# When keys are asked for, and how far behind its transfer a reciprocal stands: an attention and feed-forward kernel on Trainium2

## The chip, the cores and the metric

The kernel runs on one core of a Trainium2 chip. The metric is device time in microseconds (us), the median of some runs; one further execution is profiled. TensorE (PE in the profile) multiplies matrices, VectorE (DVE) reduces and does elementwise work, ScalarE (ACT) evaluates functions, GpSimd (POOL) does elementwise work too, and SyncE (SP) issues nearly all DMAs. Each engine works through its own list of instructions in order, and waits for the others through semaphores.

## The reference

4096 rows of width 256 go through two sandwich layers, in 32-bit floats:

```python
x = x + layernorm(attention(layernorm(x)))      # 16 heads of 16, causal softmax, projection
x = x + layernorm(ffn(layernorm(x)))
# ffn(h): silu(h @ w1.T * s1) * (h @ w2.T * s2)   256 -> 1024
#         gelu(. @ h1.T * sh1), gelu(. @ h2.T * sh2)   1024 -> 1024 twice
#         . @ w3.T * s3                                1024 -> 256
```

Attention is over all 4096 rows, each row with those up to itself. The feed-forward weights are -1, 0 or 1, with a scale for each output.

## The kernel before

**Attention in items.** The rows are cut into 8 blocks of 512 (QB), the heads into 4 groups of 4 (G). An item (j, g) is one query block with one group of heads; there are 32, in the order (0,0), (0,1) and so on. Item (j, g) has 4(j+1) steps, one for each 128 keys (`kt`), so 576 steps in all; a normal one takes about 2.7 us. A step asks for keys (`ask`), takes a pair of units of the row maxima (products `pm` L508 on TensorE, maxima L521 and L525 on DVE), two score units (products `s` L591, exponential L606 on ACT, the causal mask L611 on POOL on the diagonal), the product with the values of an earlier step (`av` L641), and then some pieces of background work. The maxima of an item are found up to two items ahead of its scores, so the `pm` products need its keys that early. The `pm` products write banks that come free only when DVE has reduced them.

**The order of the work** is written out by hand: inside a `manual_schedule`, each engine's instructions stand in the order in which the code issues them, and an engine that waits holds up all that comes behind it. The same goes for SP and its DMAs.

**Keys.** Keys and queries of a block are computed by `prep`, split into a high and a low half, and written to memory (L389, 256 KB each, from SP; the destination's outermost dimension has 8 rows of heads). For each item they are loaded again in the form that the products want. `chunks` lists all pairs (item, key block) in order; `keys` loads the next one of the list (two DMAs of 256 KB, L396) into a ring of 16 slots, each of two tiles. Chunk c of item (j, g) holds the 512 keys of block c for group g. Queries are loaded at an item's start, two items ahead.

**Background.** `prep(j + 2)` is added at step 2 of item (j, 0), `project(j)` when the last group of block j has been weighed; both are generators, and each `yield` ends a piece. `bg.pace` shares the pieces that are left out over the steps that are left; PREP, PROJECT and NORM are the numbers of pieces it counts with. A `yield Background.BESIDE` lets a further unit of maxima stand beside a background matmul. 88 pieces of weight rounding (`halve_weights`, L677 to L696) go in between.

**project(j)** (from L185) loads the block's x, and the softmax sums from the stored weighed values (L191, as soon as the last group's store, L652, has landed). Some pieces later DVE takes their reciprocal (L194), in the next piece it is stored (L196) and loaded again broadcast over the rows of a head (L200 to L204, beside the weighed values `oT`); some pieces later POOL multiplies (L208), one product in a piece; two pieces on the projection's matmuls `py` (L218), the bias on DVE (L226) and the statistics follow, then the normalisation on POOL and the store of x1 (L240).

**Feed-forward.** `feed_forward` (from L848) goes over the 8 blocks: 8 output chunks of w1 and w2 (`za`, `zb`, L940, L959, L961), then 8 chunks of h1 and 8 of h2 (`z`, L940, L974), each followed on DVE by a split into high and low halves (L910, L911), and at last w3 (`pyf`, L987). `project(7)` and after it `norm_block(1)` are background of block 0: one piece after each w1/w2 chunk, two after each h1/h2 chunk:

```python
                        bg.step()
                        if j == 0:
                            bg.step()
```

`norm_block` takes statistics (L142), adds epsilon (`ve`, L143), raises to the power -0.5 on POOL (`rstd`, L145), normalises on DVE (`yn`, L149), and in the next piece transposes on TensorE (`ptf`, L260).

Of the kernel before, what the change touches and what calls it, by code (L numbers as in the profile page):

```python
# [19 lines left out]
NT = QB // P  # L20
# [47 lines left out]
def sandwich_kernel(  # L68
# [39 lines left out]
    def rows(src, j):  # L108
        return src[j * QB : (j + 1) * QB, :].rearrange("(t p) d -> p t d", p=P)

    def load_block(j, src=x):
        t = xpool.tile([P, NT, D], F32, tag="x", name=f"x{j}")
        nc.sync.dma_start(out=t, in_=rows(src, j))
        return t
# [21 lines left out]
    def layernorm_stats(src, mv, t):  # L136
        st = stat.tile([P, nc.vector.BN_STATS_DIM], F32, tag="bn", name="bn")
        nc.vector.bn_stats(st, src)
        nc.vector.bn_aggr(mv[:, t, :], st)

    def layernorm_rstd(mv):
        ve = stat.tile([P, NT], F32, tag="ve", name="ve")  # L142
        nc.vector.tensor_scalar_add(ve, mv[:, :, 1], EPS)  # L143
        rstd = stat.tile([P, NT], F32, tag="rstd", name="rstd")
        nc.gpsimd.tensor_tensor(rstd, ve, neghalf, ALU.pow)  # L145
        return rstd

    def normalize(dst, src, mv, rstd, t, engine=nc.vector):
        engine.tensor_scalar(  # L149
            dst, src, mv[:, t, 0:1], rstd[:, t : t + 1], ALU.subtract, ALU.mult  # L150
        )
# [28 lines left out]

    weighed = [scratch.tile([G, P, QB], F32, tag=f"av_{j}", name=f"avd_{j}") for j in range(NB)]
    inverse = [scratch.tile([H, QB], F32, tag=f"inv_{j}", name=f"invd_{j}") for j in range(NB)]
    PREP, PROJECT, NORM = 22, 20, 12

    def project(j, room):  # L185

        xj = load_block(j)

        sums = stat.tile([P, H * QB // P], F32, tag="sums", name=f"sums_{j}")
        heads = weighed[j].rearrange("g (h e) n -> (g h) e n", e=HW)  # L190
        nc.sync.dma_start(out=sums, in_=heads[:, HD, :].rearrange("h (a n) -> h a n", a=8))  # L191
        for _ in range(3):
            yield True
        nc.vector.reciprocal(sums, sums)  # L194
        yield True
        nc.sync.dma_start(out=inverse[j].rearrange("h (a n) -> (h a) n", a=8), in_=sums)  # L196
        oT, inv = room.features(j)
        for c in range(DC):
            mine = slice(8 * c, 8 * (c + 1))
            nc.sync.dma_start(out=oT[:, c, :], in_=heads[mine, 0:HD, :])  # L200
            nc.sync.dma_start(
                out=inv[:, c, :],
                in_=inverse[j][mine, None, :].to_broadcast([8, HD, QB]),
            )  # L204
        for _ in range(4):
            yield True
        for c in range(DC):
            nc.gpsimd.tensor_tensor(oT[:, c, :], oT[:, c, :], inv[:, c, :], ALU.mult)  # L208
            yield True
        for _ in range(2):  # L210
            yield True
        y = room.tokens(j)
        mv = stat.tile([P, NT, 2], F32, tag="mv", name=f"mvy_{j}")
        for half in range(0, NT, 2):
            ps = room.bank(f"py_{j}_{half}").rearrange("p (t f) -> p t f", t=2)
            for t in range(2):
                for c in range(DC):
                    nc.tensor.matmul(  # L218
                        ps[:, t, :],
                        lhsT=oT[:, c, (half + t) * P : (half + t + 1) * P],  # L220
                        rhs=wp[:, c, :],
                        start=(c == 0),
                        stop=(c == DC - 1),
                    )
                yield Background.BESIDE
            nc.vector.tensor_tensor(  # L226
                y[:, half : half + 2, :],
                ps,
                bp[:, None, :].to_broadcast([P, 2, D]),
                ALU.add,  # L230
            )
            for t in range(2):
                layernorm_stats(y[:, half + t, :], mv, half + t)
            yield True
        rstd = layernorm_rstd(mv)
        for t in range(NT):
            normalize(y[:, t, :], y[:, t, :], mv, rstd, t, nc.gpsimd)
            nc.gpsimd.tensor_tensor(y[:, t, :], y[:, t, :], xj[:, t, :], ALU.add)
            yield True
        nc.sync.dma_start(out=rows(x1[j], 0), in_=y)  # L240
        yield True
# [36 lines left out]
    with ExitStack() as actx:  # L278
# [114 lines left out]
        def load_rows(tag, name, key, j, h):  # L393

            t = (piece if key == "k" else query)(tag, name, F32R)
            nc.sync.dma_start(  # L396
                out=t.bitcast(F32),
                in_=halves_of[key, j][h : h + 2].rearrange("h a b d n -> (h a b d) n"),
            )
            return t  # L400
# [11 lines left out]
        chunks = [(n, c) for n in range(G * NB) for c in range(n // G + 1)]  # L412
        RING = 2 * NB
        kT, asked = {}, [0]

        def keys(n, c):

            for pr in range(2):
                kT[n, c, pr] = load_rows(
                    f"k{asked[0] % RING}_{pr}", f"k{n}_{c}_{pr}", "k", c, 4 * (n % G) + 2 * pr  # L420
                )
            asked[0] += 1

        def ask(n, kt):

            while asked[0] < len(chunks) and chunks[asked[0]][0] <= n + 2:
                if asked[0] >= RING and chunks[asked[0] - RING] >= (n, (kt - 1) // NT):
                    return
                keys(*chunks[asked[0]])

        xTs = {}

# [189 lines left out]
        class Values:  # L622
# [9 lines left out]
            def step(self, now):  # L632
                if not self.queue or self.queue[0][0] > now:
                    return
                _, j, g, kt, q0, es = self.queue.popleft()
                last = NT * (j + 1) - 1
                if self.av is None:
                    self.av = ps_av.tile([P, QB], F32, tag="av", name=f"av_{j}_{g}")
                for h in range(4):
                    o = (4 * g + h) * VW  # L640
                    nc.tensor.matmul(  # L641
                        self.av[h * HW : (h + 1) * HW, q0:],
                        lhsT=vb[kt // NT][:, kt % NT, o : o + HW],
                        rhs=es[h // 2][:, h % 2, q0:],
                        start=(kt == 0),
                        stop=(kt == last),
                    )
                if kt == last:
                    av_sb = wk1.tile([P, QB], F32, tag="av_sb", name=f"av_sb_{j}_{g}")
                    nc.scalar.copy(av_sb, self.av)  # L650
                    self.av = None
                    nc.sync.dma_start(out=weighed[j][g], in_=av_sb)  # L652
                    if g == G - 1 and j < NB - 1:
                        bg.add(("project", j), project(j, room), PROJECT)
# [122 lines left out]
        for n, (j, g) in enumerate(items):  # L777
# [22 lines left out]
            for kt in range(count[n]):  # L800
                ask(n, kt)
                if (g, kt) == (0, 2) and j + 2 < NB:
                    bg.add(("prep", j + 2), prep(j + 2), PREP)
                due = begun + (goal - begun) * (kt + 1) // count[n] - issued
                pairs = [next(stream) for _ in range(due)]
                issued += due
                es = []
                if pairs:
                    issue(MaxUnit(*pairs[0][0]))
                es = [  # L810
                    issue(ScoreUnit(j, g, kt, pr, not pairs and next(alone)))
                    for pr in range(2)
                ]
                if pairs:
                    issue(MaxUnit(*pairs[0][1]))
                values.step(now + 1)
                for pair in pairs[1:]:
                    for args in pair:
                        issue(MaxUnit(*args))
                now += 2  # L820
                values.add(j, g, kt, max(kt - NT * j, 0) * P, es, now - 1)
                rows_of(now)
                bg.pace(count[n] - kt + count[n] * max(G - 2 - g, 0))
                if j > 0 and kt % 4 == 2 and kt < NT * j:
                    next(halving, None)
# [22 lines left out]
    def feed_forward(halves):  # L848
# [6 lines left out]
        with ExitStack() as fctx:  # L855
# [93 lines left out]
            room, bg = Room(), Background()  # L949
            keep_features(0)([xT0[:, c, :] for c in range(DC)])  # L950
            bg.add("project", project(NB - 1, room), PROJECT)
            for j in range(NB):
                xT = xTs[j]
# [91 lines left out]
```

## Time and profile before

| what | value |
|---|---|
| time, three runs | 2571.3, 2574.32, 2575.26 us; median 2574.32 |
| the profiled execution's own time | 2574.63 us |
| its span in the profile | 2572.9 us |
| PE busy | 95% |
| DVE, ACT, POOL busy | 71%, 49%, 22% |
| mean granted clock of TensorE | 0.966 |
| loads of keys, L396 | 288 of 256 KB |

The span runs from the first to the last instruction; the execution's time is 1.7 us more. Lines named L... are those of the kernel before; from L426 on the changed kernel's are two higher. In a line of the timeline stand the start and the length in us, the engine (PEld is a weight load, SPq a DMA's issue on SP), the line, the operation, output and input by name, the shapes and the number of instructions; in square brackets how long the engine had been idle before and what released it. The granted clock is the share of TensorE's full speed that its throttle gave.

### The profile page before, as it was taken

The numbers are of one execution on the slowest core, as the hardware profiler recorded it, in microseconds if no ns is written. First come the engines' busy times: TensorE is split into PE (matmuls) and PEld (weight loads), VectorE is DVE, ScalarE is ACT, GpSimd is POOL, SyncE is SP. The second block draws the span as 40 slices with busy tenths as digits, with TensorE's granted clock in tenths as the row PEclk, the third lists the DMA queues.
The fourth block names the chain that finished last, engine by engine and source line by source line (L and its number), as shares of the span: only waits on it lengthen the run. The fifth ranks groups of instructions, "written<-read, shape, count | busy, mean of one in ns | idle before, by whom it ended". The sixth has DMA issues, their size and how long they took to land. (4 is left out here: it accounts for less than half of the span.)

```text
span 2572.9 us, 40118 instructions
## 1 busy us (share of the span) xinstructions
PE 2439.2 (95%) x15237; PEld 1444.8 (56%) x15237; DVE 1824.1 (71%) x3965; ACT 1257.2 (49%) x1490; POOL 575.2 (22%) x869
## 2 busy tenths in 40 slices
PE   5899999999999999999999999999989999999998
PEld 2454445445445544554455554544468877887786
DVE  2687788879788987898899898986055445544553
ACT  1335466556566655666577666766712222222221
POOL 2325333332242234322322222000120000000000
PEclk8779899899999999999999999999999999999999
DMA  4444244232233323324212232111120000000000
GB/s 156 144 152 154 88 135 153 99 129 74 91 108 123 120 83 130 109 79 141 66 62 95 83 96 72 57 45 55 42 90 17 17 1 17 17 17 1 17 9 10
DMA packets 134777, 202.73 MB, mean 79 GB/s; under 512 B 14864, under 2 KB 59536, under 8 KB 134576
## 3 DMA queue, kind: packets, MB, share of 16 engines
q1 hardware_dynamic: 132624, 198.75, 23.3%
q8 instruction: 122, 2.00, 0.3%
q10 hardware_dynamic: 1776, 1.18, 0.2%
q0 software_dynamic: 176, 0.15, 0.1%
q14 instruction: 79, 0.65, 0.1%
HBM read 137.91 MB, written 62.13 MB: 78 GB/s over the span
## 5 line engine op out<-in xcount | busy, mean ns | idle before, releaser
L606 ACT ACTIVATE e<-s 128x1024 f32<-128x1024 f32 (+3 forms) x1175 | 1040.6, 936 | 618.5 <-PE s L591 611.5
L521 DVE TENSOR_REDUCE mx<-pm 128x1 f32<-128x512 f32 x1792 | 1112.4, 682 | 160.4 <-PE pm L508 145.8
L508 PE MATMUL pm<-k,q 64*128 64x512 f32 (+3 forms) x2304 | 636.8, 460 | 56.8 <-DVE mx L521 40.7
L508 PEld LDWEIGHTS pm<-k,q 64*128 64x128 f32 x2304 | 326.5, 190 | 567.3 <-DVE mx L521 394.7
L641 PE MATMUL av<-e,v 128*32 128x512 f32 (+3 forms) x4608 | 591.1, 584 | 2.9 <-POOL e L611 2.9
L591 PE MATMUL s<-q,k 64*128 64x512 f32 (+3 forms) x2304 | 476.3, 395 | 7.6 <-DVE y L226 3.1
L591 PE MATMUL s<-mrow,ones 64*128 64x512 f32 (+3 forms) x2304 | 461.6, 384 | 0.0
L525 DVE CUSTOM_DVE_ANT_0 pm<-pm,mask 128x384 f32<-128x384 f32 (+3 forms) x512 | 239.8, 517 | 75.3 <-PE pm L508 71.4
L974 ACT ACTIVATE fb<-z,sh 128x512 f32<-128x512 f32 x128 | 88.1, 688 | 396.6 <-PE z L940 377.8
L591 PEld LDWEIGHTS s<-q,k 64*128 64x128 f32 x2304 | 237.0, 191 | 79.0 <-issue 19.3
L591 PEld LDWEIGHTS s<-mrow,ones 64*128 64x128 f32 x2304 | 241.8, 191 | 38.6 <-DVE mrow L565 0.7
L611 POOL TENSOR_SCALAR_AFFINE_SELECT e<-e 128x256 f32<-128x256 f32 x256 | 102.2, 407 | 647.6 <-ACT e L606 645.9
L145 POOL TENSOR_TENSOR rstd<-ve,neghalf 128x4 f32<-128x4 f32 x32 | 32.9, 1027 | 847.7 <-DVE ve L143 822.1
L940 PE MATMUL z<-hb_0h,h 128*128 128x512 f32 x512 | 203.7, 398 | 0.0
L940 PE MATMUL z<-hb_0l,h 128*128 128x512 f32 x512 | 202.2, 395 | 0.0
L641 PEld LDWEIGHTS av<-e,v 128*32 128x32 f32 x4608 | 92.6, 109 | 148.8 <-issue 130.0
L910 DVE CAST hb_1h<-fb 128x512 fp32r<-128x512 f32 x64 | 27.4, 428 | 149.9 <-ACT fb L974 149.9
L910 DVE CAST hb_0h<-fb 128x512 fp32r<-128x512 f32 x64 | 27.5, 430 | 139.4 <-ACT fb L974 139.4
L940 PEld LDWEIGHTS z<-hb_0h,h 128*128 128x128 f32 x512 | 96.8, 189 | 22.9
L940 PEld LDWEIGHTS z<-hb_0l,h 128*128 128x128 f32 x512 | 96.8, 189 | 22.1
L959 ACT ACTIVATE sl<-za,s 128x512 f32<-128x512 f32 x64 | 44.1, 689 | 131.4 <-DVE fa L961 66.4
L693 POOL CAST wh<-wc 128x256 fp32r<-128x256 f32 x88 | 34.9, 397 | 261.8 <-DMA wc<-in_h_t_dram 197.1
(235 smaller groups left out, 2430.9 us busy)
## 6 DMA issues: line engine op xcount, KB each, us to landing
k<-k SPq DMA_DIRECT2D x288, 256.0 KB
q<-q SPq DMA_DIRECT2D x64, 256.0 KB
x<-in_x_dram SPq DMA_DIRECT2D x16, 512.0 KB
k<-hik SPq DMA_DIRECT2D x32, 256.0 KB
k<-lok SPq DMA_DIRECT2D x32, 256.0 KB
q<-hiq SPq DMA_DIRECT2D x32, 256.0 KB
q<-loq SPq DMA_DIRECT2D x32, 256.0 KB
avd<-av_sb SPq DMA_DIRECT2D x32, 256.0 KB
```

Source lines behind the costliest of these rows:

```text
L508: nc.tensor.matmul(ps[:, 0:n], lhsT=qT[j, g][pr][r, t * P : (t + 1) * P], rhs=kT[G * j + g, c, pr][r, 0:n], start=True, stop=True,)
L521: nc.vector.tensor_reduce(self.mx[:, h, c : c + 1], ps[:, 0:n], AX.X, ALU.max)
L525: nc.vector.tensor_tensor_reduce(out=ps[:, 0:n], in0=ps[:, 0:n], in1=mask[:, QB - n : QB], scale=1.0, scalar=-3.0e38, op0=ALU.add, op1=ALU ...
L591: nc.tensor.matmul(self.ps[i][:, self.q0 :], lhsT=(self.k, ones[pr])[m][r, :], rhs=(qT[j, g][pr], mT[j, g])[m][r, self.q0 :], start=(m == ...
L606: nc.scalar.activation(e[:, at : at + n, q0:], ps[:, :, q0:], AF.Exp)
L611: nc.gpsimd.affine_select(out=at, in_=at, compare_op=ALU.is_ge, fill=0.0, base=0, pattern=[[0, 2], [1, P]], channel_multiplier=-1,)
L641: nc.tensor.matmul(self.av[h * HW : (h + 1) * HW, q0:], lhsT=vb[kt // NT][:, kt % NT, o : o + HW], rhs=es[h // 2][:, h % 2, q0:], start=(k ...
L693: nc.gpsimd.tensor_copy(hi, w)
L910: nc.vector.tensor_copy(hi, full)
L940: nc.tensor.matmul(ps, lhsT=w[c], rhs=single(part[:, c, :]), start=(c == 0 and i == 0), stop=(c == kc - 1 and i == parts - 1),)
L959: nc.scalar.activation(sl, za, AF.Silu, scale=s1[:, oc : oc + 1])
L974: nc.scalar.activation(h, z, AF.Gelu, scale=sc[:, oc : oc + 1])
```

## The change

`ask` no longer asks at each step for all chunks that the ring and the limit of two items ahead allow; it asks at even steps alone, and for one chunk. In `project`, two more pieces stand between the load of the sums and the reciprocal, and one more between the loads of the weighed values and the product; PROJECT counts the three.

```diff
-    PREP, PROJECT, NORM = 22, 20, 12
+    PREP, PROJECT, NORM = 22, 23, 12
...
         nc.sync.dma_start(out=sums, in_=heads[:, HD, :].rearrange("h (a n) -> h a n", a=8))
-        for _ in range(3):
+        for _ in range(5):
             yield True
         nc.vector.reciprocal(sums, sums)
         yield True
...
-        for _ in range(4):
+        for _ in range(5):
             yield True
         for c in range(DC):
             nc.gpsimd.tensor_tensor(oT[:, c, :], oT[:, c, :], inv[:, c, :], ALU.mult)
             yield True
...
         def ask(n, kt):
 
-            while asked[0] < len(chunks) and chunks[asked[0]][0] <= n + 2:
-                if asked[0] >= RING and chunks[asked[0] - RING] >= (n, (kt - 1) // NT):
-                    return
-                keys(*chunks[asked[0]])
+            at = asked[0]
+            if kt % 2 or at == len(chunks) or chunks[at][0] > n + 2:
+                return
+
+            if at < RING or chunks[at - RING] < (n, (kt - 1) // NT):
+                keys(*chunks[at])
```

## The prediction

> **What bounds it now.** First the page's busy row, then the list of waits, then the timeline around those waits.
>
> ```profile
> PE 2439.2 (95%) x15237; PEld 1444.8 (56%) x15237; DVE 1824.1 (71%) x3965; ACT 1257.2 (49%) x1490; POOL 575.2 (22%) x869
> ```
>
> TensorE works 95% of the span, so only what shortens or makes a TensorE gap, or slows its clock, moves the end. The waits that touch the edit:
>
> ```profile
> DVE sums L194 <- DMA sums<-avd: 21.0, 7, 7.6
> PE pm L508 <- DVE mx L521: 40.7, 62, 3.9
> ```
>
> (Columns: total us, count, longest.) The reciprocal waits 21.0 us for its transfer, and TensorE waits for DVE's maxima. Block 6 shows that they are one thing:
>
> ```profile
> 1189.52 0.32 SPq L652 DMA_DIRECT2D avd<-av_sb  x1
> ...
> 1194.17 0.39 PE L508 MATMUL pm<-k,q 64*128 64x512 f32 x1
> ...
> 1194.71 0.58 SPq L191 DMA_DIRECT2D sums<-avd  x1
> ...
> 1197.29 0.55 DVE L194 RECIPROCAL sums<-sums 128x64 f32<-128x64 f32 x1 [4.46 <-DMA sums<-avd]
> ...
> 1198.44 0.79 PE L508 MATMUL pm<-k,q 64*128 64x512 f32 x1 [3.88 <-DVE mx L521]
> ```
>
> The sums are read only once the last group's store has landed; DVE stands 4.46 us at the reciprocal, the pm banks behind it stay full, and TensorE stands 3.88. The like stands at 280.6, 447.5, 654.5 and 904.5 us: 3.36+1.09+2.45+0.86+3.88 = 11.6 us. The clock drops afterwards:
>
> ```profile
> 653.00:667.00 14.00, 11.55 (x66) 5.07 (x68) 7.62 (x20) 5.98 (x7) 4.86 (x6) 0.76 0.52 169
> 1192.00:1206.00 14.00, 10.12 (x60) 4.70 (x60) 7.19 (x16) 5.77 (x7) 3.99 (x5) 0.76 0.66 197
> ```
>
> (Window, us, busy PE, PEld, DVE, ACT, POOL, then granted clock, DMA share, GB/s.) A clock of 0.76 over 14 us is 3.4 us lost in each; 280 to 292 has 0.86, 1.7 us. Part lies in the gaps themselves: against 2.7 us of a normal step, the steps at these places are 19.5 us too long together, 7 to 8 beyond the gaps. I take 7.0, a choice between 4 and 8.5.
>
> [...] 0.50 in the slices after 1194, while the 0.86 us gap costs no clock. [...]
>
> **The change, part by part.** All engines keep their program order, so the built order tells where things land.
>
> *Reciprocal two pieces later, in attention.* It moves 8 to 9 DVE instructions down for five of the seven projections, 13 and 6 for two, and 4 for the first: about two steps, 5.4 us. The longest wait is 4.46, so all vanish: +11.6 us, and the clock +7.0. The second (447) could keep up to 1 us. Cover is the maxima and stats between; without it the 4.46 stays. The product, one piece later again, waits on POOL (22% busy) for its transfer; the y matmuls come three pieces later and x1 is needed much later: nothing.
>
> *The same in the last projection, in the feed-forward.*
>
> ```profile
> 1874.30 0.40 PE L940 MATMUL zb<-xTf_0l,w 128*128 128x512 f32 x1
> ...
> 1876.94 0.55 DVE L194 RECIPROCAL sums<-sums 128x64 f32<-128x64 f32 x1 [7.63 <-DMA sums<-avd]
> ...
> 1878.12 0.51 PE L940 MATMUL z<-ha_0h,h 128*128 128x512 f32 x1 [3.42 <-DVE fa L961]
> ```
>
> The sums land at about 1876.9 behind weights whatever DVE does. Two more w1/w2 chunks (DVE .75+.43+.69 = 1.87 us each) go first: the wait is 7.63-3.74 = 3.9, and TensorE's 3.42 gap, with its clock loss, goes: +3.7. Further on:
>
> ```profile
> 1924.38 1.03 POOL L145 TENSOR_TENSOR rstd<-ve,neghalf 128x4 f32<-128x4 f32 x1 [12.27 <-DVE ve L143]
> ...
> 1926.01 2.21 PE L260 MATMUL ptf<-ident,yn 128*128 128x128 f32 x8 [3.75 <-DVE yn L149]
> ```
>
> In block 0 two pieces run after each h1/h2 chunk. Normalising is piece 27 and the transposes 28, in one pair, so nothing covers rstd 1.03 plus four yn of .35. Three pieces later they are 30 and 31, in different pairs: a chunk of 3.7 us (16 matmuls of .23) comes between, against a chain of 4.4 (activation .69, casts .43+.69, ve .16, rstd 1.03, yn 1.4) to 5.0 with stats of .6 ahead of it: 0.7 to 1.3 stay, I take 1.1. Lost before: 3.75, about 1.2 of the slow 2.21 [...], and 1 of clock after it = 5.9. +4.8. If both pieces fell in one pair again, nothing would be gained here.
>
> *Keys asked for by one chunk in every second step.* Before, an item's first step asks for all that the ring allows up to two items ahead. Comparing each load's place in SP's order with its first use, all later chunks keep 10 us or more of lead, save these.
>
> Place A, item (0,2). The second chunk of (1,0) is asked for at step 0 before (106 us, ahead of prep(2)'s writes); after, at step 2, behind 12 of them. In TensorE's order its first product comes right after pq.
>
> ```profile
> 120.55 1.88 PE L366 MATMUL pq<-xT,wqk 128*128 128x512 f32 x4
> ...
> 122.36 0.33 PE L508 MATMUL pm<-k,q 64*128 64x128 f32 x2
> ...
> 125.90 2.98 SPq L389 DMA_DIRECT2D q<-hiq  x2
> ...
> 128.97 2.50 SPq L389 DMA_DIRECT2D q<-loq  x2
> ```
> ```profile
> 120.00:138.00 18.00, 17.06 (x101) 9.51 (x99) 8.67 (x29) 7.66 (x13) 7.85 (x12) 1.00 0.52 194
> 138.00:158.00 20.00, 18.80 (x79) 9.30 (x77) 15.14 (x46) 4.08 (x7) 2.44 (x6) 0.50 0.57 199
> ```
>
> TensorE is there at 122.4. SP gets to the keys at 131.5. The 12 writes are 3.15 MB; at 194 to 200 GB/s, begun at 117 and slow at first, they are through at 135.5; [...] Lower bound: landing 2 us after issue, 133.5, 11.1. Clock after it: an estimate of 3 (0 to 6), from the 3.4 lost after 3.88. A smaller one: (1,1)'s second chunk behind the store of 140.88, 1 us (0 to 2).
>
> Place B, item (1,2). The third chunk of (2,0) comes behind four writes of prep(3), its product directly after one that TensorE has before:
>
> ```profile
> 225.36 0.50 PE L508 MATMUL pm<-k,q 64*128 64x512 f32 x2
> ...
> 226.86 1.25 SPq L389 DMA_DIRECT2D k<-hik  x2
> ...
> 228.21 1.81 SPq L389 DMA_DIRECT2D k<-lok  x2
> ```
>
> TensorE is there at 225.8; SP is free at 230.0; the 1.05 MB (2-us slices at 97, 195, 175, 202 GB/s) are through at 234.6, the keys at 236.4: 10.6 us, at least 7.7, and the clock 2. The last chunk of (3,0) lands 0.5 us before its use: 0.5. POOL, DVE and ACT stand with TensorE at A and B; no work is left that could fill the gap, since the order is fixed.
>
> Sum: +11.6+7.0+3.7+4.8 = 27.1 gained; 15.1+3+1+10.6+2+0.5 = 32.2 lost; 5.1 slower. The profiled execution is 2574.63 (span 2572.9 and 1.7 around it), 0.3 over the median 2574.32: 2579.7 against it, **2579.4** on the median. A measurement tells about 0.2%, 5.1 us, from no change, so this lies at the edge.
>
> **Rivals.**
> *R1, the keys don't queue (faster).* [...] if the keys go round them, A is 11.1 and B 7.7, and if DVE, not TensorE's clock, paces the steps behind (15.14 of 20 us busy already), no clock is lost. 27.1-11.1-7.7-1.5 = 6.8: 2567.5. It decides once A and B with their clock are under 20.5 us together. For it: the share of 0.52; [...] Chance 0.25.
> *R2, the stall resets the clock (same).* 138 to 158 ran at 0.50 though TensorE was busy. If the stall shifts this to full clock, DVE bounds the stretch: 20-15.1 = 4.9 back, 2574.5. Nothing tells which way. 0.13.
> *R3, the gains are smaller (slower).* The half clock after A stays a further 6 us' worth and half of the 11.8 that I count for clock and transposes (7.0+4.8) fails to come: 2579.4+6+5.9 = 2591. 0.15.
> That the reciprocals don't move is excluded by the built order; that the keys come earlier elsewhere helps no wait in the list.
>
> **Numbers.** Main case 0.47, its own range 2570 to 2590 (A 11 to 16, B 7.7 to 10.6, clocks 0 to 10). The range 2565 to 2593 takes in all. Faster: most of R1 and a sliver of the main, 0.26. Same: R2, the rest of R1 and the lower part of the main, 0.25. Slower: 0.49.
>
> **What would show it.** A wait of pm for k of about 15 us ending near 137, and one of about 10 ending near 255 (236.4, shifted by the 19 of A); sums waits left in the feed-forward only, about 3.9; no gap over 1 us before ptf; full clock where blocks 3 and 6 had 0.76. Wrong, if TensorE starts pm at A within 2 us of SP's issue, if no such wait is listed, or if new sums waits stand later in the DVE order.

## The result, and the profile after

The changed kernel takes 2590.99 us (median of six runs, 2588.78 to 2596.05) against 2575.3 of the kernel before beside it: a ratio of 1.0066, 95% interval 1.0053 to 1.0079, 15.7 us slower. Forecast were 2579.4 in the likeliest case, and 2565 to 2593. The profiled execution has a span of 2588.8 us, 15.9 over that of before. The page's busy row and the list of waits (the same columns) of the changed kernel:

```profile
PE 2435.3 (94%) x15237; PEld 1443.8 (56%) x15237; DVE 1826.4 (71%) x3965; ACT 1257.7 (49%) x1490; POOL 574.4 (22%) x869
```
```profile
PE pm L510 <- DMA k<-k: 31.2, 4, 15.9
...
PEld pm L510 <- DMA k<-k: 16.7, 1, 16.7
...
DVE bn L138 <- DMA x<-in_x_dram: 4.8, 1, 4.8
...
DVE sums L194 <- DMA sums<-avd: 3.0, 1, 3.0
```

TensorE is busy nearly as long as before (2435.3 for 2439.2), so the time lies between its instructions. The wait for the sums fell from 21.0 to 3.0 us; a wait of TensorE for keys of 31.2 has come (15.9 and 11.6 at places A and B, 2.9 in the first 100 us, and 0.9 at 429.71 for the last chunk of (3,0)), and a wait of DVE for the rows `x`. Place A and place B in the timeline of the changed kernel:

```profile
121.75 1.88 PE L366 MATMUL pq<-xT,wqk 128*128 128x512 f32 x4
...
129.98 2.71 SPq L389 DMA_DIRECT2D q<-loq  x2
132.75 2.07 SPq L396 DMA_DIRECT2D k<-k  x2
139.52 0.47 PE L510 MATMUL pm<-k,q 64*128 64x128 f32 x2 [15.89 <-DMA k<-k]
...
257.53 0.50 PE L510 MATMUL pm<-k,q 64*128 64x512 f32 x2
...
260.38 1.82 SPq L389 DMA_DIRECT2D k<-lok  x2
262.24 1.59 SPq L396 DMA_DIRECT2D k<-k  x2
269.59 0.48 PE L510 MATMUL pm<-k,q 64*128 64x128 f32 x2 [11.56 <-DMA k<-k]
```

SP issues the two key loads only after the writes, and TensorE, which has done nothing but wait since the product ahead of them, starts when they land. After A it works at half clock at first (columns of the windows as in the prediction):

```profile
139.50:146.30 6.80, 6.78 (x25) 3.37 (x26) 1.37 (x9) 1.08 (x2) 0.81 (x2) 0.50 0.00 0
```

The windows that answer to the two of before (columns as there) lie around the reciprocals at 695.89 and 1232.99:

```profile
685.00:699.00 14.00, 14.00 (x108) 7.42 (x110) 12.43 (x27) 10.10 (x11) 2.73 (x4) 1.00 0.61 182
1225.00:1239.00 14.00, 14.00 (x110) 7.29 (x108) 12.22 (x28) 10.06 (x11) 2.72 (x4) 1.00 0.73 227
```

TensorE is busy throughout, at full clock. In the feed-forward, DVE's wait is 3.04 us and the gap ahead of `ptf` 0.70:

```profile
1901.16 0.55 DVE L194 RECIPROCAL sums<-sums 128x64 f32<-128x64 f32 x1 [3.04 <-DMA sums<-avd]
...
1950.92 1.64 PE L260 MATMUL ptf<-ident,yn 128*128 128x128 f32 x8 [0.70 <-DVE yn L149]
```

Where the two traces stand against each other, read at the first score product of an item: at (2,0) the changed kernel is 42.2 us late (1.1 of it came before item (0,2), while the first rows and weights arrive). Its feed-forward begins at 1882.29 against 1857.38, 24.9 late, so blocks 2 to 7 gave 17.3 back; it ends 15.9 late, so the feed-forward gave back 9.0. The forecast had 18.6 and 8.5 for these two, and 32.2 for what the keys lose. Blocks 0 and 1 lose 10 us more than it said.

One new wait was not in it. In block 1 of the changed kernel's timeline:

```profile
225.97 0.73 POOL L698 TENSOR_TENSOR fit<-fit,wc 128x256 f32<-128x256 f32 x1
...
228.00 0.73 POOL L238 TENSOR_TENSOR y<-y,x 128x256 f32<-128x256 f32 x1
...
228.75 0.37 SPq L240 DMA_DIRECT2D x<-y  x1
229.17 0.51 SPq L113 DMA_DIRECT2D x<-in_x_dram  x1
...
233.74 0.43 DVE L138 BATCH_NORM_STATS2 bn<-x 128x6 f32<-128x256 f32 x1 [4.81 <-DMA x<-in_x_dram]
...
234.89 0.48 PE L510 MATMUL pm<-k,q 64*128 64x256 f32 x1 [3.43 <-DVE mx L527]
```

project(0) now ends three pieces later, and a piece of weight rounding (L695 to L698 there, 3.0 us of POOL from 223.71 to 226.70) stands between POOL's last two normalisations. So SP's store of x1 waits longer, and behind it in SP's list stands the load of `x` for prep(3). DVE's statistics come three pieces after that load, find it under way, and stand 4.81 us; TensorE stands 3.43 behind DVE. Before, the same rounding followed the last normalisation, and DVE waited 1.33 us there.

### The profile page after: what moved, and what is told of

Read it like the earlier page. It is cut to its first block, busy times and chain, and to the rows that moved or that the text cites. A ratio compares the mean times of both kernels' runs of the same rounds, so it can differ in the third digit from the quotient of the medians.

```text
span 2588.8 us, 40115 instructions
## 1 busy us (share of the span) xinstructions
PE 2435.3 (94%) x15237; PEld 1443.8 (56%) x15237; DVE 1826.4 (71%) x3965; ACT 1257.7 (49%) x1490; POOL 574.4 (22%) x869
## 5 line engine op out<-in xcount | busy, mean ns | idle before, releaser
L510 PE MATMUL pm<-k,q 64*128 64x512 f32 (+3 forms) x2304 | 631.9, 459 | 76.7 <-DMA k<-k 31.2
L695 POOL CAST wh<-wc 128x256 fp32r<-128x256 f32 x88 | 34.9, 397 | 305.3 <-DMA wc<-in_h_t_dram 221.9
```

Source lines behind the costliest of these rows:

```text
L510: nc.tensor.matmul(ps[:, 0:n], lhsT=qT[j, g][pr][r, t * P : (t + 1) * P], rhs=kT[G * j + g, c, pr][r, 0:n], start=True, stop=True,)
```

## The experiments

The kernel before was timed beside each group: 2575.07 us for e1 to e4, 2573.12 for e5 to e8, 2572.59 for e9 and e10. Runs of different groups are compared by how far each stands from the kernel before beside it. Each run has one trace. Where two traces are compared at item (2,0), what they differ by before item (0,2), where the edits begin to act, is taken off. e2_project and e3_early do the same work in between and still differ by 2.1 us there, so a figure from one pair of traces is no surer than that.

**The two parts apart.** e1_keys has the new `ask` and the old `project`. With the old pacing one unit of maxima comes before its chunk was asked for, so it is asked for there:

```diff
+                while (G * j + g, c, pr) not in kT:
+                    keys(*chunks[asked[0]])
```

> Only the new way of asking for keys, project as before (one chunk, the third of (2,0), is asked for at its first use, since the maxima get there a piece earlier). Theory K (late keys cost the time, the later reciprocals give back some 26): stalls of pm for k of about 16 and 11 us, the waits of DVE for the sums still there: about 2603, 28 over before. Rival Q (the keys cost only some 12, because the half clock that follows them had been there before, and project's later pieces bring new waits that eat their gain): about 2587.

e2_project is the changed kernel with the old `ask`:

> Only project's three later pieces, keys asked for as before. The order on TensorE, DVE, ACT and POOL is that of the changed kernel; only SP's differs, so the difference to the changed kernel is what the keys cost. K: 2562, 13 under before; no wait of pm for k after 100 us, the wait of DVE for x in block 1 (4.8 us in the changed kernel) still there. Q: 2579.

Measured: e1_keys 2599.48 (ratio 1.0087, 1.0058 to 1.0116), 24.4 over before; e2_project 2556.55 (0.9925, 0.9907 to 0.9942), 18.5 under it. The changed kernel and e2_project differ in SP's order alone, so the keys cost it 34 us (2590.99-2556.55). Theory K holds, and Q falls. One point of K missed: in e1_keys the waits for the sums are not all still there, its list has 10.6 us of the 21.0. In the trace of e2_project there is no wait for k after 100 us, and the one for `x` is there:

```profile
DVE bn L138 <- DMA x<-in_x_dram: 5.3, 1, 5.3
```

It is 9.9 us late at (2,0) (0.9 of it from before item (0,2)), and its feed-forward begins 9.2 us early: 19.0 given back in blocks 2 to 7, then 8.6 in the feed-forward.

But -18.5 and +24.4 add up to +5.9, not +15.7. The last run, e10_keys_only_late, takes that up.

**Which keys.** e3_early is the changed kernel, with this at the head of `ask`; e7_keysA has `n < 4` in place of `n < 8`:

```diff
+            while n < 8 and asked[0] < len(chunks) and chunks[asked[0]][0] <= n + 2:
+                if asked[0] >= RING and chunks[asked[0] - RING] >= (n, (kt - 1) // NT):
+                    return
+                keys(*chunks[asked[0]])
```

> The changed kernel, with keys asked for as before during the first eight items, and one chunk in every second step from then on. K: only the chunks of (1,0) and (2,0) are late, so the same as with project alone, 2562 within 3. If the one chunk at a time costs something later too, it stands 3 or more above project alone; if it helps there, 3 or more below. Q: 2579 or more.

> The changed kernel, with keys asked for as before during the first four items only: the chunk of (1,0) is early again, that of (2,0) stays late. If the stall in item (0,2) costs its own length and some clock: 2591-20 = 2571, and the wait of pm for k of 11 us near 240 stays. If the clock gives part back, as in the 20 us at half clock that the kernel before has there: 2578 or more.

e3_early took 2557.29 (0.9935, 0.9916 to 0.9955), as e2_project: all that the keys cost, they cost in the first eight items, and afterwards one chunk at a time neither costs nor gains beside the later reciprocals, as far as four runs between 2550 and 2562 tell. e7_keysA took 2568.71 (0.9982, 0.9970 to 0.9994; its runs spread over 2557 to 2583), 4.4 under the kernel before; its wait at B stays, 12.9 us. The changed kernel stands 15.7 over and e2_project 18.5 under, so place A was worth 20.1 us to the changed kernel and place B 14.1. By the traces at (2,0) they are 18.1 and 14.1: A is the changed kernel against e7_keysA, B is e7_keysA against e2_project. So the stall at A costs its own 15.9 and some 2 to 4 us more. The 6.8 us at half clock after it are 3.4 of slow clock; the clock gave nothing back.

**The wait for x.** e4_x_early is the changed kernel with the load of block 3 issued when prep(3) is added; e5_project_x is e2_project with the same lines:

```diff
                 if (g, kt) == (0, 2) and j + 2 < NB:
+                    if j == 1:
+                        xb[j + 2] = load_block(j + 2)
```

> The changed kernel, with the rows x of block 3 loaded when prep(3) is added and not when it starts, so that the load doesn't stand in SP's list behind the store of x1 of block 0. Theory X (the wait of 4.8 us on DVE comes from that store, which waits for POOL): the wait goes, TensorE's gap of 3.4 near 233 goes, 2585 to 2588. Rival (DVE would have waited for something else there, or the clock decides): 2590 or more.

> Project's three later pieces, keys asked for as before, and the rows x of block 3 loaded when prep(3) is added. Theory X (of project's later pieces, all but the wait for x in block 1 is gain): the wait of DVE for x (5.3 us with project alone) goes, with TensorE's gap of 2.1 and some clock: 2551, 5 under project alone. Rival Y (block 1 loses its 8 us by the later order on POOL as such, x or not): 2556 to 2558.

e4_x_early took 2585.7 (1.0043, 1.0031 to 1.0054), 5.3 under the changed kernel; its executions spread over 2577.7 to 2597.4, so by itself it only fits. e5_project_x took 2551.46 (0.9909, 0.9891 to 0.9928), 21.7 under the kernel before where e2_project is 18.5 under: 3.1 better. Times so close don't tell X from Y by themselves, since the intervals overlap. In neither trace does DVE wait for `x`, and at (2,0) the traces gain 5.1 and 3.3. So theory X holds: that load costs 3 to 5 us.

e6_first is e2_project with project(0) as it was:

```diff
-        for _ in range(5):
+        for _ in range(5 if j else 3):
...
-        for _ in range(5):
+        for _ in range(5 if j else 4):
...
-                        bg.add(("project", j), project(j, room), PROJECT)
+                        bg.add(("project", j), project(j, room), PROJECT if j else 20)
```

> As project alone, but project(0) keeps the pieces it had (3 and 4, 20 in all); keys as before. X and Y both: block 1 runs as before and its loss of 8 goes, 2548.5. If it is 2555 or more, the loss in block 1 is not from project(0).

It took 2547.77 (0.9907, 0.9889 to 0.9926), 25.4 under the kernel before, 6.8 better than e2_project; its trace gains 8.7 at (2,0), of the 9.0 that e2_project loses there. So nearly all of block 1's loss comes with the later project(0), and the load of `x` is 3 to 5 us of it. What the rest is no run here takes apart; e5_project_x still has a gap of 1.86 in which the values' products wait for the mask on POOL, where the later normalisations stand.

**Two pieces or three.** e8_recip has five pieces ahead of the reciprocal, four ahead of the product, PROJECT 22, and the old `ask`.

> Two pieces more ahead of the reciprocal and none more ahead of the product (22 pieces in all), keys as before. By the count of pieces, normalising and transposing of block 1 in the feed-forward fall in one pair again: TensorE's gap of 3.7 before ptf is back and 4 to 5 us with it, while the sums' gap stays away: 2556.5+4.5 = 2561, if attention is the same. If the third piece is worth nothing there: 2556.5. If the wait for x in block 1 needs three pieces and goes with two: up to 8 less, which the trace would show at 200 to 220.

Measured 2549.99 (0.9905, 0.9886 to 0.9923): 11 under the first number, nearest to the last case. Both halves are in its trace. With two pieces the last normalisation comes ahead of the rounding:

```profile
206.50 0.75 POOL L238 TENSOR_TENSOR y<-y,x 128x256 f32<-128x256 f32 x1
207.18 0.41 POOL L693 CAST wh<-wc 128x256 fp32r<-128x256 f32 x1
207.27 0.37 SPq L240 DMA_DIRECT2D x<-y  x1
207.69 0.51 SPq L113 DMA_DIRECT2D x<-in_x_dram  x1
...
212.56 0.43 DVE L138 BATCH_NORM_STATS2 bn<-x 128x6 f32<-128x256 f32 x1 [0.55 <-DMA x<-in_x_dram]
...
1909.31 1.96 PE L260 MATMUL ptf<-ident,yn 128*128 128x128 f32 x8 [3.74 <-DVE yn L149]
```

and the gap ahead of `ptf` is back to 3.74. Its feed-forward begins at 1841.02 against e2_project's 1848.22, 7.2 earlier, and it ends 2.8 earlier: by these traces the third piece is worth 4.4 us in the feed-forward, and costs up to 7.2 in attention.

e9_best takes for each block what stood best: project(0) with 3 and 4 pieces (20), 1 to 6 with 5 and 4 (22), 7 with 5 and 5, and the old `ask`:

```diff
-        for _ in range(5):
+        for _ in range(5 if j else 3):
...
-        for _ in range(5):
+        for _ in range(5 if j == NB - 1 else 4):
...
-                        bg.add(("project", j), project(j, room), PROJECT)
+                        bg.add(("project", j), project(j, room), 22 if j else 20)
```

> Keys as before; project(0) as before (3 and 4 pieces), project(1) to project(6) with 5 and 4, project(7) with 5 and 5. Each is the choice that stood best in the runs so far: no halving of weights comes between POOL's last two normalisations in block 1 (no wait of DVE for x), no wait for the sums in attention, and normalising and transposing in different pairs in the feed-forward. From the run with 5 and 4 throughout, 2550: 4.4 less in the feed-forward, 2545.5; from the one with project(0) as before, 2547.8: up to 4 less in blocks 4 and 5. If the third piece is worth nothing in the feed-forward: 2550.

It took 2545.79 us (0.9898, 0.9881 to 0.9916; 26.8 under the kernel before beside it), the lowest median of all; that it is below e6_first, 25.4 under, the intervals don't tell. Its waits are not all gone: DVE still stands 2.0 us for `x` in block 1 and 1.5 for the sums in attention.

**Why the parts don't add up.** e10_keys_only_late is the kernel before with e3_early's `ask`:

> Project as before; keys asked for as before during the first eight items, and one chunk in every second step from then on. Theory O (with fewer keys queued ahead, the last group's store and the sums come earlier, so that the keys' part of the change takes away some of the waits that project's part takes away too, and the two gains overlap by about 10 us): the wait of DVE for the sums falls from 21 us to 8 to 12, 2575-9 = 2565. Rival (the two add up, and the difference of 10 came from elsewhere): 2574 to 2576.

Measured 2558.58 (0.9949, 0.9933 to 0.9965), 14.0 under before. Its list of waits has

```profile
DVE sums L194 <- DMA sums<-avd: 12.5, 4, 7.5
```

with 7.5 of it the feed-forward's (before: 7.6 of 21.0), so the sums' wait in attention fell from 13.4 to 5.0. SP's list shows why. First project(1) in the kernel before, then in this one:

```profile
271.19 3.77 SPq L396 DMA_DIRECT2D k<-k  x6
...
280.68 0.58 SPq L191 DMA_DIRECT2D sums<-avd  x1
```
```profile
272.50 0.92 SPq L396 DMA_DIRECT2D k<-k  x2
...
278.85 0.58 SPq L191 DMA_DIRECT2D sums<-avd  x1
```

The last group's store is issued in between, at 275.06 and at 276.37, and the load of the sums waits for it to land. In the kernel before that takes 5.6 to 6.2 us in project(1) to project(4), behind six to ten key loads; in this one 2.2 to 2.5, behind two. In project(5), where eight loads of weights (L174) stand ahead of the store in both, it is 5.2 and 5.1. Theory O holds: the sums' wait fell to about what it said, and the time fell further, by 14.0 for 9. By the trace 14.2 of the gain lie in the items (2,0), (3,0) and (4,0), in which project(1) to project(3) run, so it comes with these waits. TensorE's gaps behind them account for some 6 of it; that the rest is the slow clock that followed them (granted 0.98 for 0.97 from (2,0) to (5,0)) is argued, not shown. The two edits take away the same waits, and what one has taken is not there for the other.

## Why the prediction was right or wrong

*Right in sign and range, its likeliest case 11 us too low.* The sum of gains and losses, step by step:

*Reciprocals in attention, +11.6 and +7.0 of clock:* right, as a sum. 17.3 in the changed kernel, 19.0 in e2_project, the waits gone (0.9 us is left in e2_project) and the clock whole where it was 0.76. How much of it is clock no run takes apart. What was not seen is that either edit alone brings part of it: "that the keys come earlier elsewhere helps no wait in the list" looked only at the keys, but keys that are asked for later let the store and the sums come earlier, and e10_keys_only_late gains 14.0 us by that. It did not spoil the sum, since the waits can be removed only once.

*Feed-forward, +3.7 and +4.8:* right. 9.0 and 8.6 measured; DVE's wait 3.04 for 3.9, the `ptf` gap 0.70, and e8_recip shows the pairing of pieces, worth 4.4. The forecast took 1.2 of the transposes' 2.21 us (clock 0.65) for slowness; at full clock, at 1950.92 in the changed kernel, they took 1.64, so it is 0.6.

*Place A, 15.1+3, and the smaller one, 1:* right. A stall of 15.89, and 18.1 in all by the traces, 20.1 by the medians. *Place B, 10.6+2:* right, slightly low: 11.56, and 14.1 in all. *The last chunk of (3,0), 0.5:* 0.87. R1 falls, since A and B cost far more than 20.5 together: the loads landed 4.7 and 5.8 us after SP had issued them (134.82 to 139.52, 263.83 to 269.59), not 2 us, the time from the end of the sums' issue to the reciprocal at 1197.29 in the kernel before. The lengths forecast for the stalls, 15.1 and 10.6, were the author's estimates: when keys land that are asked for behind such writes, the trace of the kernel before doesn't show, nor which of the 16 engines the writes held (the share of 0.52 is a mean over all). In the changed kernel the share was 0.51 to 0.53 in each us from 130 to 134, while SP issued the last writes of A and the keys, and 0.86 and 0.87 from 135 to 137; what held the loads is not shown. R2 falls too: after A the clock is 0.61 from 156 to 182, and nothing came back. The half clock lasted 6.8 and 6.4 us of work after A and B, and as long, 6.8 us, in the kernel before after a gap of 2.45 us at 656.97.

*The step that failed:* "the y matmuls come three pieces later and x1 is needed much later: nothing". x1 isn't needed soon, but its store stands in SP's list ahead of the load of `x` for prep(3), which is. With project alone block 1 loses 7 to 9 us (e6_first by medians and trace), 3 to 5 of them by that load (e4_x_early and e5_project_x), nearly all of them with the later project(0). The built order had been read for DVE's rows and for SP's key loads, not for what POOL does ahead of x1's store and what SP has behind it. In the traces that is 9.0; A and B are 32.2 together for 31.7 forecast; blocks 2 to 7 give back 17.3 for 18.1 (the reciprocals' 18.6 less 0.5 for the last chunk of (3,0)); 1.1 lies ahead of item (0,2), where no edit had begun to act; and the feed-forward gives back 0.5 more. That makes up, but for rounding, the 10.8 that the sum of 5.1 misses of 15.9. So most of the miss is this one term. That the result stayed in the range was luck as far as this term goes: the range had been made wide for other reasons. R3's time, 2591, was met, though not in R3's way: the gains came nearly whole.

## What to carry to other kernels

A piece of background work that is moved takes its whole chain along: follow its last store in the DMA queue and ask what load stands behind it, and what other work falls between its steps on another engine (here 3.0 us of rounding on POOL). Before a load is asked for later, see whether a burst of writes enters the same queue in between; here two late chunks, four of 288 loads, cost 32 to 34 us, and the others a wait of 0.9. When two edits aim at one queue, time each alone: here, with the keys of the first items asked for as before, the one is worth 14.0 us alone, the other 18.5, and both together 17.8.

## What the runs showed of the hardware

Two key loads of 256 KB, issued behind the halves' writes, had landed 4.7 us (A) and 5.8 us (B) after their issue had ended, when TensorE's product began. The DMA engines were not idle for most of that time: their share, in steps of 1 us, was 0.47 or more until 138 at A and 0.43 or more until 268 at B, and fell below that only in the last 1.5 and 1.6 us (0.11 and 0.22).

After TensorE's stall of 15.9 us the granted clock stayed at 0.50 for the first 6.8 us of work (139.5 to 146.3), after the one of 11.6 us for 6.4 (269.6 to 276). A gap of 2.45 us in the kernel before was followed by half clock too, one of 0.85, at 905.39, was not (clock 1.00 to 910). And a busy TensorE is not always at full clock: in the changed kernel it was 0.50 from 164 to 180, with TensorE busy for 15.2 of the 16 us and no gap over 0.4; the kernel before shows the like from 138 to 158.
